# A two-layer adaLN and attention kernel: PSUM tiles dealt anew, bias products on all 128 rows, and a triangular W1 W1^T

## The chip, the cores and the metric

The kernel runs on one core of a Trainium2 chip, in one launch. The metric is the device time of that launch in microseconds (us). The profile's names are used for the engines: PE (TensorE, matrix products; PEld is its weight load), DVE (VectorE), ACT (ScalarE), POOL (GpSimd), SP (the engine whose queue issues the transfers). L905 is line 905 of the kernel. The matrix products write to PSUM, which has eight banks of 128 x 512 float32; a "PSUM tile" below is one bank. A "pass" is one matrix product with one set of weights.

## The reference, cut to what matters

The input x is 128 sequences of 64 tokens with 256 features. Layer 0 is a gated recurrence over the 64 tokens followed by a feed-forward with 8-bit fake quantisation. Layer 1 is attention and a feed-forward in hyperbolic space, modulated by a condition (adaLN), then a linear map with 6-bit block quantisation:

```python
h_new = jnp.tanh(h * leak + sigmoid(h @ Wh.T + z_t @ Wz.T + b) * z_t)      # layer 0, 64 steps
h = _act_fake_quant(jax.nn.silu(gate) * up, clip_down[0])                   # layer 0, feed-forward
x = x + jnp.einsum('bsi,hi->bsh', h, _weight_fake_quant(w_down))
...
xm = expmap0(layer_norm(logmap0(x)) * (1 + sc_msa) + sh_msa)                # layer 1, attention
q, k, v = (_to_heads(plin(xm, w, b)) for w, b in ((w_q, b_q), (w_k, b_k), (w_v, b_v)))
attn = jax.nn.softmax(einsum('bhqd,bhkd->bhqk', qt, kt) / sqrt(HD))         # 16 heads of 16
x = mobius_add(x, expmap0(g_msa * logmap0(plin(_from_heads(out_h), w_o, b_o))))
xm = expmap0(layer_norm(logmap0(x)) * (1 + sc_mlp) + sh_mlp)                # layer 1, feed-forward
ff = plin(plin(xm, w_f1, b_f1), w_f2, b_f2)
x = mobius_add(x, expmap0(g_mlp * logmap0(ff)))
...
xd = mx_dequant(mx_quant(x)); out = xd @ wd.T + bias; return x_layer0 + out
```

plin(x) is expmap0(logmap0(x) @ w + b): a linear map whose result is scaled row by row by a function of its norm. The kernel uses that for the inner plin(xm, w_f1, b_f1): the norm of u W1 + b1 is u G u^T + 2 u W1 b1 + b1 b1, with G = W1 W1^T, a symmetric 256 x 256 matrix. So the 1024-wide middle is never formed: one product with the 512 columns [G | W1 W2] gives both the norm and the result.

## The kernel before, in words

The 8192 tokens are 64 tiles of 128. Three stages follow each other. First comes the scan of the recurrence (up to about 210 us), in whose gaps the generators pieces() and products() prepare the weights: products() computes G and W1 W2 on PE and copies them from PSUM (L344), and split() stores each in two parts, so that a product is made in three passes of the float32r type. Second comes the feed-forward of layer 0 (to 308 us), which writes its hidden values to memory. Third comes the loop of fused(), which takes groups of 4 tiles, as two pairs (h2 = 0, 1), through stages that work on different groups at a time:

- front (L844): loads the hidden values, rounds them, multiplies them with w_down in PSUM tile dn (L872), adds x (L874, L875) and takes the row statistics. The product's inner length of 704 is five chunks of 128 rows and a half chunk of 64 (j = 5).
- norms (L1089): layer-norm coefficients (L656 ff.) for the attention of one group and the feed-forward of another together, then modulate (L706) and clip_ball (L720, L610).
- attention (L880): transposes of u into a qk tile, uT in two parts (L897, L898); q, k, v for two tiles in qk tiles of 512 and 256 columns (L905 the bias, L908 the six passes), copied by ACT (L910); norms of the heads (L912 to L925); scaling on POOL (L934, L938); transposes and scores in sc tiles (L959, arrays of 64 x 64), exp on ACT (L967); the result in ao (L974, 128 x 64), divided on DVE (L978, L979); transposes and the product with w_o in ao again (L1000, read by L1004).
- mlp (L1010): transposes and the product with [G | W1 W2] in ml tiles (L1026 the bias, L1029 the passes), read by DVE (L1032, the norm) and ACT (L1035, the result).
- tail (L1119): the Moebius additions of both halves (L789).
- fp6 (L1048): block quantisation, transposes and the last product in fp tiles (L1081 the bias, L1083), read by DVE (L1086).

Bias rows are added by a product of ones with the bias split into three bfloat16 rows. ones3 has 67 rows and rows3 too: the biases lie at rows 0 to 2, 32 to 34 and 64 to 66, and such a product uses 3 rows of the array.

The eight PSUM banks of the loop are two tiles for qk, two for sc, and one each for ao, ml, fp and dn. bank() takes one by its tag. The order of each engine's instructions is not the program's: a scheduler places them when the kernel is built, by priorities, dependences and the tiles that are free, and then it is fixed; each engine works its own list in order. LA = 5 and LM = 3 are the number of groups by which attention runs ahead and the last stage behind.

Of the kernel before, what the change touches and what calls it, by code (L numbers as in the profile page):

```python
# [11 lines left out]
F32 = mybir.dt.float32  # L12
F32R = mybir.dt.float32r
BF16 = mybir.dt.bfloat16
# [8 lines left out]
P = 128  # L23
B, T, D = 128, 64, 256
# [18 lines left out]
NG = NT // GN  # L43
AR = 8
TS = 4
CFG = {'rnd': 'S', 'ef': 8, 'fill': {'x1a': 'V', 'mod0': 'V'}, 'hold': [3, 0], 'mk': 3, 'mv': 6, 'xs': 3, 'la': 3, 'sb': 7, 'qks': 'GGGG', 'deq': 'VV', 'first': 1000, 'hb': 2, 'q_h': 'P', 'q_x1': 'P', 'q_xr': 'P', 'q_ot': 'P', 'q_out': 'P', 'q_ada': 'P', 'room': [[0.3, 0.3, 0.55], [0.5, 0.4, 0.2]], 'qv': 64, 'p1': 'GVGVGVGV', 'x1': 3, 'u1': 16, 'u2': 6, 'qkv': 2, 'sq': 1, 'uT1': 2, 'uT2': 2, 'qM': 2, 'kT': 2, 'e': 4, 'oT': 1, 'yT': 1, 'hq': 2, 'hl': 2, 'xr': 1, 'ot': 2, 'ada00': 2, 'ada02': 2, 'ada10': 2, 'ada12': 4, 'dn': 1, 'qk': 2, 'sc': 2, 'ao': 1, 'ml': 1, 'fp': 1, 'mod0': 'GGGV', 'mod1': 'VVVV', 'sqm0': 'SSSS', 'sqm1': 'SSSS', 'su0': 'VVVV', 'su1': 'VGVG', 'q8': 'GGGGGG', 'hqc': 'SSSVVV', 'qm': 'SSSS', 'x1a': 'GV', 'gate0': 'GGGG', 'gate1': 'GGGG', 'yb': 'GG', 'va': 'GGGG', 'sqt': 'SSSS', 'sqg': 'SSSS', 'sqo': 'SSVS', 'f2e': 'SSSS', 'early': 0, 'q8f': 'VVVVVV', 'hqf': 'SSSVVV', 'fl': 1, 'un': 2, 'jsu': 1, 'LA': 5, 'LM': 3, 'tl': 6, 'ord': 1, 'xt': 3, 'q_xt': 'P'}
GT = 4
NGR = NTILE // GT

# [21 lines left out]
def tile_kernel(ctx, tc, a, out):  # L71
# [21 lines left out]

    ones = const.tile([P, P], F32, name="ones")
    V.memset(ones, 1.0)
    ones3 = const.tile([67, P], BF16, name="ones3")
    V.memset(ones3, 1.0)

    mhead = const.tile([P, 4], F32, name="mhead")
    V.tensor_reduce(mhead, ident.rearrange("p (j v d) -> p v j d", v=4, d=HD), AX.XY, ALU.add)  # L100

    wt = ctx.enter_context(tc.tile_pool(name="wt", bufs=1))
    wqkv = wt.tile([P, 2, 2, 3 * D], F32R, name="wqkv")
    wm = wt.tile([P, 2, 2, 2 * D], F32R, name="wm")
    wo = wt.tile([P, 2, D], F32, name="wo")
    wfT = wt.tile([P, 2, D], F32, name="wfT")
# [2 lines left out]
    bf2 = wt.tile([P, D], F32, name="bf2")  # L109
    bb2 = wt.tile([P, 1], F32, name="bb2")  # L110

    rows3 = wt.tile([67, 2 * D], BF16, name="rows3")
    sdh = wt.tile([P, D], F32, name="sdh")
    cu = wt.tile([P, 1], F32, name="cu")

# [20 lines left out]
    with ExitStack() as l0:  # L136
# [15 lines left out]
        with ExitStack() as sc_:  # L152
# [173 lines left out]
            def products():  # L326

                b1T = setup.tile([P, 8], F32, name="b1T")
                dma(out=b1T, in_=a["b_f1T"])
                s1 = stage2([P, 8, D], a["w_f1T"].rearrange("(c p) k -> p c k", p=P))
                s2 = stage2([P, 8, D], a["w_f2"].rearrange("(c p) k -> p c k", p=P))
                r2 = setup.tile([1, 2 * D], F32, name="r2")
                for w, s_ in ((0, s1), (1, s2)):
                    pt = bank()
                    for c in range(2):
                        for k in range(8):
                            PE.matmul(pt[:, c * D : (c + 1) * D], lhsT=s1[:, k, c * P : (c + 1) * P],  # L340
                                      rhs=s_[:, k, :], start=(k == 0), stop=(k == 7))
                            yield 0, 0, 0.43
                    gst = setup.tile([P, 2, D], F32, name="gst", tag="gst", bufs=2)
                    S.copy(gst.rearrange("p c k -> p (c k)"), pt)  # L344
                    yield 0, 0.52, 0
                    for c in range(2):
                        sl = slice(w * D, (w + 1) * D)
                        split((wm[:, 0, c, sl], wm[:, 1, c, sl]), gst[:, c, :])
                        yield 0, 0.35, 0
                    pt = bank()  # L350
                    for k in range(8):
                        PE.matmul(pt[:1, :D], lhsT=b1T[:, k : k + 1], rhs=s_[:, k, :], start=(k == 0), stop=(k == 7))
                        yield 0, 0, 0.43
                    S.activation(r2[:, w * D : (w + 1) * D], pt[:1, :D], AF.Copy, scale=2.0 - w)
                    yield 0, 0.3, 0
                for i, part in enumerate(split3(r2, 1, G_)):
                    dma(out=rows3[64 + i : 65 + i, :], in_=part)
                bsq = setup.tile([P, 8], F32, name="bsq")
                bs1 = setup.tile([P, 1], F32, name="bs1")
                S.activation(bsq, b1T, AF.Square, accum_out=bs1)  # L360
                pt = bank()
                PE.matmul(pt[:, :1], lhsT=ones, rhs=bs1, start=True, stop=True)
                V.tensor_copy(bb2, pt[:, :1])
                yield 0.15, 0.3, 0.1


                for w in range(2):
                    st = stage2([P, 2, 3 * D], a["w_ada"].rearrange("(c p) k -> p c k", p=P)[:, :, w * 3 * D : (w + 1) * 3 * D])
                    ba = setup.tile([P, 3 * D], F32, name="ba", tag="ba", bufs=1)
                    dma(out=ba, in_=a["b_ada"][w * 3 * D : (w + 1) * 3 * D].partition_broadcast(P))  # L370
                    for q in range(3):
                        sl = slice(q * D, (q + 1) * D)
                        pt = bank()
                        for k in range(2):
                            PE.matmul(pt[:, :D], lhsT=h0T[:, k, :], rhs=st[:, k, sl], start=(k == 0), stop=(k == 1))
                            yield 0, 0, 0.43
                        if q == 1:
                            V.scalar_tensor_tensor(ba[:, sl], pt[:, :D], 1.0, ba[:, sl], ALU.add, ALU.add)
                        else:
                            V.tensor_tensor(ba[:, sl], pt[:, :D], ba[:, sl], ALU.add)  # L380
                        yield 0.35, 0, 0
                    dma(out=ada_d[:, :, w * 3 * D : (w + 1) * 3 * D],
                        in_=ba.unsqueeze(1).broadcast_to((P, AR, 3 * D)))
# [159 lines left out]
def fused(ctx, tc, a, out_tok, x_tok, L):  # L543
# [44 lines left out]
            es = CFG["fill"].get(key, es)  # L588
        return es[g % len(es)]

    def bank(tag):
        return ps.tile([P, 512], F32, name=tag, tag=tag, bufs=CFG[tag])

    def big(tag, shape, dt=F32):
        return pl.tile(shape, dt, name=tag, tag=tag, bufs=CFG[tag])
# [248 lines left out]
    def front(i):  # L844
# [4 lines left out]
        for h2 in pairs:  # L849
            pr = i0 // 2 + h2  # L850
            early = pr < CFG["early"]
            grp = pr // 2
            hs_ = slice((grp % 2) * 64, (grp % 2) * 64 + 64)
            hl = hls.pop(0)
            hq = big("hq", [P, 6, 2 * P], BF16)
            q8 = big("hb", [P, 6, 2 * P], I8)

            for e, r, j in runs("q8f" if early else "q8", hs_):
                scale(e, q8[r, j, :], hl[r, j, :], cu[r])
            for e, r, j in runs("hqf" if early else "hqc", hs_):  # L860
                if e == "V":
                    V.tensor_copy(hq[r, j, :], q8[r, j, :])
                else:
                    S.copy(hq[r, j, :], q8[r, j, :])
            load_h(pr + CFG["hl"])
            xr = big("xr", [P, 2, D])
            move("xr", out=xr, in_=x_tok[:, i0 + 2 * h2 : i0 + 2 * h2 + 2, :])
            py = bank("dn")
            for i in range(2):
                for j in range(6):  # L870
                    r = slice(0, P) if j < 5 else hs_
                    PE.matmul(py[:, i * D : (i + 1) * D], lhsT=hq[r, j, i * P : (i + 1) * P], rhs=wdT[r, j, :],  # L872
                              start=(j == 0), stop=(j == 5))
            V.tensor_tensor(x1.t[h2], two(py), bc_out(sdh, 2), ALU.mult)  # L874
            ENG[pick("x1a", h2)].tensor_tensor(x1.t[h2], x1.t[h2], xr, ALU.add)  # L875
            for g in (2 * h2, 2 * h2 + 1):
                stats(mv1[:, g, :], x1[g], 1)
            move("x1", out=x1_d[:, i0 + 2 * h2 : i0 + 2 * h2 + 2, :], in_=x1.t[h2])

    def attention(i, u, sums):  # L880
# [4 lines left out]
        for h2 in pairs:  # L885
# [13 lines left out]
            for xy in range(2):  # L899
                cs = slice(xy * P, (xy + 1) * P)  # L900
                for lo, hi in ((0, 512), (512, 768)):
                    pm = bank("qk")
                    n_ = hi - lo
                    o3 = slice(0, 3) if lo == 0 else slice(32, 35)
                    PE.matmul(pm[:, :n_], lhsT=ones3[o3, :], rhs=rows3[o3, :n_], start=True, stop=False)  # L905
                    for k in range(2):
                        for q, (w, z) in enumerate(PASSES):
                            PE.matmul(pm[:, :n_], lhsT=uT[:, z, k, cs], rhs=wqkv[:, w, k, lo:hi],  # L908
# [101 lines left out]
    def mlp(i, u, x2, sums):  # L1010
# [3 lines left out]
        for h2 in pairs:  # L1014
# [8 lines left out]
            for i in range(2):  # L1023
                g = 2 * h2 + i
                pm = bank("ml")
                PE.matmul(pm, lhsT=ones3[64:67, :], rhs=rows3[64:67, :], start=True, stop=False)  # L1026
                for k in range(2):
                    for q, (w, z) in enumerate(PASSES):
                        PE.matmul(pm, lhsT=uT[:, z, k, i * P : (i + 1) * P], rhs=wm[:, w, k, :],  # L1029
                                  start=False, stop=(k == 1 and q == 2))  # L1030
                junk3 = pl.tile([P, D], BF16, name="junk3", tag="junkz", bufs=1)
                V.tensor_tensor_reduce(out=junk3, in0=pm[:, :D], in1=u[g], scale=1.0, scalar=0.0,  # L1032
# [15 lines left out]
    def fp6(i, av, s2):  # L1048
# [4 lines left out]
        for h2 in pairs:  # L1053
# [24 lines left out]
            pm = bank("fp")  # L1078
            for i in range(2):
                o = pm[:, i * D : (i + 1) * D]  # L1080
                PE.matmul(o, lhsT=ones3[32:35, :], rhs=rows3[32:35, D:], start=True, stop=False)  # L1081
                for c in range(2):
                    PE.matmul(o, lhsT=yT[:, 2 * i + c, :], rhs=wfT[:, c, :], start=False, stop=(c == 1))  # L1083
            ot = big("ot", [P, 2, D])
# [132 lines left out]
```

## Time and profile before

| | |
|---|---|
| three runs | 1404.55, 1413.27, 1414.75 us; median 1413.27 |
| profiled execution | 1410.42 us, span 1408.5 us, mean granted PE clock 0.859 |
| scan of layer 0 | 0 to 210 us: PE busy 185.1, DVE 132.7, ACT 92.5 us |
| feed-forward of layer 0 | 210 to 308 us: PE 82.6, DVE 97.4, ACT 85.6 us |
| fused loop | 308 to 1408.5 us: PE 915.7, DVE 914.7, POOL 726.7, ACT 637.5 us |
| first and last use of ao by L974 | 398.8 and 1248.7 us |
| PE, L908 x768 | 199.4 us, mean 390 ns |
| PE, L1029 x384 | 122.6 us, mean 457 ns |
| PE, the bias products L905 x128, L1026 x64, L1081 x64 | 45.7, 26.8, 20.0 us |
| PE, L872 x384 | 72.3 us, mean 315 ns |

A row of a group gives its busy time (overlaps counted once) and the mean length of one instruction. Products on PE overlap, so their mean length is longer than the distance between their starts; the timeline gives the starts. The chain of work that ended last is followed back from the last instruction, at each step to what released it. A wait is put down to the event that ended it. The granted clock is the share of PE's full clock that the chip allowed.

### The profile page before, as it was taken

The numbers are of one execution on the slowest core, as the hardware profiler recorded it, in microseconds if no ns is written. First come the engines' busy times: TensorE is split into PE (matmuls) and PEld (weight loads), VectorE is DVE, ScalarE is ACT, GpSimd is POOL, SyncE is SP. The second block draws the span as 40 slices with busy tenths as digits, with TensorE's granted clock in tenths as the row PEclk, the third lists the DMA queues.
The fourth block names the chain that finished last, engine by engine and source line by source line (L and its number), as shares of the span: only waits on it lengthen the run. The fifth ranks groups of instructions, "written<-read, shape, count | busy, mean of one in ns | idle before, by whom it ended". The sixth has DMA issues, their size and how long they took to land.

```text
span 1408.5 us, 23861 instructions
## 1 busy us (share of the span) xinstructions
PE 1183.5 (84%) x7372; PEld 748.0 (53%) x7380; DVE 1144.8 (81%) x3604; ACT 815.5 (58%) x2363; POOL 836.6 (59%) x1043
## 2 busy tenths in 40 slices
PE   7999977974699988999889988799996999785655
PEld 4656542322466655656556565556664666553433
DVE  5666669986687988979989789979889888788863
ACT  2545447972377766667656666667765756643331
POOL 3111108865688769776685776867758764645541
PEclk9999979985599987989879899889987969976675
DMA  7113145779534234341354231532314132222111
GB/s 230 53 53 92 59 198 206 273 253 301 166 118 127 94 103 134 109 135 46 101 151 146 81 115 43 158 116 77 102 39 136 49 119 68 82 73 93 60 45 45
DMA packets 119304, 163.64 MB, mean 116 GB/s; under 512 B 10885, under 2 KB 72074, under 8 KB 119178
## 3 DMA queue, kind: packets, MB, share of 16 engines
q1 hardware_dynamic: 119178, 162.13, 36.4%
q8 instruction: 58, 0.95, 0.3%
q14 instruction: 68, 0.56, 0.1%
HBM read 115.94 MB, written 46.14 MB: 115 GB/s over the span
## 4 chain that ended last, share of the span: by engine, by line
DVE 40%; PE 35%; POOL 10%; DMA 7%; ACT 4%; issue 4%; SPq 0%; POOLq 0%; DVEq 0%; ACTq 0%
DMA ada<-ada_d 4%; PE pg L426 4%; PE qk L908 4%; PE fp L1083 4%; DVE u L789 4%; PE pg L407 3%; PE sc L959 3%; PE ml L1029 2%; PE ao L974 2%; DVE nh L913 2%; DVE bn L695 2%; DVE u L716 2%; DVE junk L735 2%; DVE u L610 2%; DVE u L1041 2%
## 5 line engine op out<-in xcount | busy, mean ns | idle before, releaser
L601 ACT ACTIVATE junk<-u 128x256 bf16<-128x256 f32 x432 | 182.2, 424 | 143.0 <-DVE u L717 46.2
L908 PE MATMUL qk<-wqkv,uT 128*128 128x512 f32 (+1 forms) x768 | 199.4, 390 | 6.3 <-DVE uT L898 3.5
L729 POOL TENSOR_TENSOR u<-u,ada 128x256 f32<-128x256 f32 x128 | 101.1, 792 | 91.7 <-ACT junk L601 88.6
L908 PEld LDWEIGHTS qk<-wqkv,uT 128*128 128x128 f32 x768 | 129.9, 207 | 46.5 <-issue 12.4
L959 PE MATMUL sc<-qM,kT 64*64 64x256 f32 x1024 | 126.7, 437 | 9.7 <-ACT kT L949 6.1
L974 PE MATMUL ao<-va,e 128*64 128x34 f32 x2048 | 93.3, 248 | 35.4 <-DVE u L979 15.3
L1029 PE MATMUL ml<-wm,uT 128*128 128x512 f32 x384 | 122.6, 457 | 0.0
L974 PEld LDWEIGHTS ao<-va,e 128*64 128x64 f32 x2048 | 83.5, 163 | 62.5 <-issue 36.3
L608 ACT ACTIVATE qM<-sc,mhead 128x256 f32<-128x256 f32 x256 | 101.3, 492 | 21.3 <-PE sc L92 21.1
L872 PE MATMUL dn<-wdT,hq 128*128 128x256 bf16 (+1 forms) x384 | 72.3, 315 | 41.3 <-DVE x L874 16.5
L938 POOL TENSOR_TENSOR va<-qkv,comb 64x256 f32<-64x256 f32 x128 | 87.2, 682 | 30.1 <-PE ao L974 24.3
L1029 PEld LDWEIGHTS ml<-wm,uT 128*128 128x128 f32 x384 | 75.5, 212 | 53.5 <-issue 35.0
L505 POOL TENSOR_TENSOR hv<-uv,sil 128x512 f32<-128x512 f32 x44 | 57.4, 1308 | 70.8 <-DVE am L508 52.2
L1083 PE MATMUL fp<-wfT,yT 128*128 128x256 f32 x256 | 92.6, 491 | 0.0
L967 ACT ACTIVATE e<-sc 128x512 f32<-128x512 f32 x128 | 73.3, 596 | 24.5 <-PE sc L959 15.1
L910 ACT COPY qkv<-qk 128x512 f32<-128x512 f32 (+1 forms) x128 | 61.3, 498 | 44.4 <-PE qk L908 43.6
L601 ACT ACTIVATION_READ_ACCUMULATOR junk<-u 128x1 f32 x432 | 86.1, 199 | 0.0
L426 PE MATMUL pg<-hsT,WT 128*128 128x128 f32 x504 | 76.3, 292 | 10.8 <-ACT hsT L438 10.4
L934 POOL TENSOR_TENSOR qkv<-qkv,comb 128x512 f32<-128x512 f32 x64 | 70.4, 1117 | 23.7 <-DVE comb L925 9.3
L426 PEld LDWEIGHTS pg<-hsT,WT 128*128 128x128 f32 x504 | 66.1, 195 | 33.3 <-ACT hsT L438 31.1
L959 PEld LDWEIGHTS sc<-qM,kT 64*64 64x64 f32 x1024 | 55.5, 147 | 48.3 <-issue 17.3
L612 POOL TENSOR_SCALAR hb<-hl,cu 128x1280 int8<-128x1280 f32 x64 | 64.8, 1018 | 23.0 <-DMA hl<-h_d 14.3
(282 smaller groups left out, 3129.7 us busy)
## 6 DMA issues: line engine op xcount, KB each, us to landing
ada<-ada_d SPq DMA_DIRECT2D x128, 256.0 KB, 3.5
h_d<-hv SPq DMA_DIRECT2D x80, 256.0 KB, 2.1
hl<-h_d SPq DMA_DIRECT2D x32, 640.0 KB, 5.1
ada<-ada_d SPq DMA_DIRECT2D x128, 128.0 KB, 2.6
xt<-in_xT_dram SPq DMA_DIRECT2D x16, 512.0 KB, 4.1
xr<-in_x_dram SPq DMA_DIRECT2D x32, 256.0 KB, 3.7
x_d<-x SPq DMA_DIRECT2D x32, 256.0 KB, 2.4
xt<-x_d SPq DMA_DIRECT2D x32, 256.0 KB, 2.7
```

The costliest lines, as they stand in the source:

```text
L426: lp = PE.matmul(pg[c][:, st], lhsT=WT[:, k, c * P : (c + 1) * P], rhs=hp[:, k, :], start=False, stop=False, skip_group_check=True)
L601: S.activation(junk, src, AF.Square, accum_out=acc)
L608: S.activation(dst, src, AF.Copy, scale=by)
L729: ENG[pick(f"gate{which}", g)].tensor_tensor(av, av, gb, ALU.mult)
L872: PE.matmul(py[:, i * D : (i + 1) * D], lhsT=hq[r, j, i * P : (i + 1) * P], rhs=wdT[r, j, :], start=(j == 0), stop=(j == 5))
L908: PE.matmul(pm[:, :n_], lhsT=uT[:, z, k, cs], rhs=wqkv[:, w, k, lo:hi], start=False, stop=(k == 1 and q == 2))
L938: ENG[pick("va", g)].tensor_tensor(va[r, :, s, 0:HD], qkv[r, xy, 512:768].rearrange("p (h d) -> p h d", d=HD), bc_in(comb[r, xy * 48 + 32 ...
L959: PE.matmul(sc[rr][s * T : (s + 1) * T, c * 256 : (c + 1) * 256].rearrange("p (v t) -> p v t", v=4), lhsT=kTs[xy][r, c, s * T : (s + 1) * ...
L967: S.activation(e.rearrange("p c v t -> p (c v t)"), sc[rr], AF.Exp, scale=1.0 / math.sqrt(HD))
L974: PE.matmul(pv[xy * T : (xy + 1) * T, hh], lhsT=E[2 * xy + hh // 4][:, c, hh % 4, :], rhs=vas[(2 * h2 + xy) % 4][:, c * 8 + hh], start=Tru ...
L1029: PE.matmul(pm, lhsT=uT[:, z, k, i * P : (i + 1) * P], rhs=wm[:, w, k, :], start=False, stop=(k == 1 and q == 2))
L1083: PE.matmul(o, lhsT=yT[:, 2 * i + c, :], rhs=wfT[:, c, :], start=False, stop=(c == 1))
```

## The change

The diff, with the long dictionary of settings cut to the entries that differ:

```diff
-CFG = {... 'dn': 1, 'qk': 2, 'sc': 2, 'ao': 1, 'ml': 1, 'fp': 1, ...}
+CFG = {... 'qk': 2, 'sc': 2, 'ao': 2, 'm': 2, ...}
...
-    ones3 = const.tile([67, P], BF16, name="ones3")
-    V.memset(ones3, 1.0)
+    ones3 = const.tile([P, 3, P], BF16, name="ones3")
+    V.memset(ones3, 0.0)
+    for n in range(3):
+        V.memset(ones3[32 * n : 32 * n + 3, n, :], 1.0)
...
-    rows3 = wt.tile([67, 2 * D], BF16, name="rows3")
+    rows3 = wt.tile([P, 2 * D], BF16, name="rows3")
+    V.memset(rows3, 0.0)
...
                     S.copy(gst.rearrange("p c k -> p (c k)"), pt)
-                    yield 0, 0.52, 0
+                    if w == 0:
+                        S.activation(gst[:, 0, P:], pt[:, P:D], AF.Copy, scale=2.0)
+                    yield 0, 0.52 + 0.3 * (1 - w), 0
...
-    def bank(tag):
-        return ps.tile([P, 512], F32, name=tag, tag=tag, bufs=CFG[tag])
+    def bank(name):
+        tag = "m" if name in ("ml", "fp", "dn") else name
+        return ps.tile([P, 512], F32, name=name, tag=tag, bufs=CFG[tag])
...
-            for i in range(2):
-                for j in range(6):
-                    r = slice(0, P) if j < 5 else hs_
-                    PE.matmul(py[:, i * D : (i + 1) * D], lhsT=hq[r, j, i * P : (i + 1) * P], rhs=wdT[r, j, :],
-                              start=(j == 0), stop=(j == 5))
+            for i, j in [(i, j) for i in range(2) for j in range(5)] + [(0, 5), (1, 5)]:
+                r = slice(0, P) if j < 5 else hs_
+                PE.matmul(py[:, i * D : (i + 1) * D], lhsT=hq[r, j, i * P : (i + 1) * P], rhs=wdT[r, j, :],
+                          start=(i == 0 and j == 0), stop=(j == 5), skip_group_check=True)
...
-                    o3 = slice(0, 3) if lo == 0 else slice(32, 35)
-                    PE.matmul(pm[:, :n_], lhsT=ones3[o3, :], rhs=rows3[o3, :n_], start=True, stop=False)
+                    PE.matmul(pm[:, :n_], lhsT=ones3[:, lo // 512, :], rhs=rows3[:, :n_], start=True, stop=False)
...
-                PE.matmul(pm, lhsT=ones3[64:67, :], rhs=rows3[64:67, :], start=True, stop=False)
+                PE.matmul(pm, lhsT=ones3[:, 2, :], rhs=rows3, start=True, stop=False)
                 for k in range(2):
+                    cs = slice(k * P, 2 * D)
                     for q, (w, z) in enumerate(PASSES):
-                        PE.matmul(pm, lhsT=uT[:, z, k, i * P : (i + 1) * P], rhs=wm[:, w, k, :],
+                        PE.matmul(pm[:, cs], lhsT=uT[:, z, k, i * P : (i + 1) * P], rhs=wm[:, w, k, cs],
                                   start=False, stop=(k == 1 and q == 2))
...
-                PE.matmul(o, lhsT=ones3[32:35, :], rhs=rows3[32:35, D:], start=True, stop=False)
+                PE.matmul(o, lhsT=ones3[:, 1, :], rhs=rows3[:, D:], start=True, stop=False)
```

In words: the eight banks become two each for qk, sc and ao, and two ("m") that ml, fp and dn share. The weights of the bias products are zero outside the three rows of their bias, so the products use all 128 rows. In front, the ten products with whole chunks come first and the two half chunks after them. G is symmetric: its upper right quarter is doubled when it is copied, and the passes of the second half of u (k = 1) leave out the lower left quarter, so they have 384 columns and not 512. The scheduler works on the changed program, so the order on every engine is another too.

More of the change, by code (lines that the diff above doesn't have):

```diff
@@ L45 @@
 TS = 4
-CFG = {'rnd': 'S', 'ef': 8, 'fill': {'x1a': 'V', 'mod0': 'V'}, 'hold': [3, 0], 'mk': 3, 'mv': 6, 'xs': 3, 'la': 3, 'sb': 7, 'qks': 'GGGG', 'deq': 'VV', 'first': 1000, 'hb': 2, 'q_h': 'P', 'q_x1': 'P', 'q_xr': 'P', 'q_ot': 'P', 'q_out': 'P', 'q_ada': 'P', 'room': [[0.3, 0.3, 0.55], [0.5, 0.4, 0.2]], 'qv': 64, 'p1': 'GVGVGVGV', 'x1': 3, 'u1': 16, 'u2': 6, 'qkv': 2, 'sq': 1, 'uT1': 2, 'uT2': 2, 'qM': 2, 'kT': 2, 'e': 4, 'oT': 1, 'yT': 1, 'hq': 2, 'hl': 2, 'xr': 1, 'ot': 2, 'ada00': 2, 'ada02': 2, 'ada10': 2, 'ada12': 4, 'dn': 1, 'qk': 2, 'sc': 2, 'ao': 1, 'ml': 1, 'fp': 1, 'mod0': 'GGGV', 'mod1': 'VVVV', 'sqm0': 'SSSS', 'sqm1': 'SSSS', 'su0': 'VVVV', 'su1': 'VGVG', 'q8': 'GGGGGG', 'hqc': 'SSSVVV', 'qm': 'SSSS', 'x1a': 'GV', 'gate0': 'GGGG', 'gate1': 'GGGG', 'yb': 'GG', 'va': 'GGGG', 'sqt': 'SSSS', 'sqg': 'SSSS', 'sqo': 'SSVS', 'f2e': 'SSSS', 'early': 0, 'q8f': 'VVVVVV', 'hqf': 'SSSVVV', 'fl': 1, 'un': 2, 'jsu': 1, 'LA': 5, 'LM': 3, 'tl': 6, 'ord': 1, 'xt': 3, 'q_xt': 'P'}
+CFG = {'rnd': 'S', 'ef': 8, 'fill': {'x1a': 'V', 'mod0': 'V'}, 'hold': [3, 0], 'mk': 3, 'mv': 6, 'xs': 3, 'la': 3, 'sb': 7, 'qks': 'GGGG', 'deq': 'VV', 'first': 1000, 'hb': 2, 'q_h': 'P', 'q_x1': 'P', 'q_xr': 'P', 'q_ot': 'P', 'q_out': 'P', 'q_ada': 'P', 'room': [[0.3, 0.3, 0.55], [0.5, 0.4, 0.2]], 'qv': 64, 'p1': 'GVGVGVGV', 'x1': 3, 'u1': 16, 'u2': 6, 'qkv': 2, 'sq': 1, 'uT1': 2, 'uT2': 2, 'qM': 2, 'kT': 2, 'e': 4, 'oT': 1, 'yT': 1, 'hq': 2, 'hl': 2, 'xr': 1, 'ot': 2, 'ada00': 2, 'ada02': 2, 'ada10': 2, 'ada12': 4, 'qk': 2, 'sc': 2, 'ao': 2, 'm': 2, 'mod0': 'GGGV', 'mod1': 'VVVV', 'sqm0': 'SSSS', 'sqm1': 'SSSS', 'su0': 'VVVV', 'su1': 'VGVG', 'q8': 'GGGGGG', 'hqc': 'SSSVVV', 'qm': 'SSSS', 'x1a': 'GV', 'gate0': 'GGGG', 'gate1': 'GGGG', 'yb': 'GG', 'va': 'GGGG', 'sqt': 'SSSS', 'sqg': 'SSSS', 'sqo': 'SSVS', 'f2e': 'SSSS', 'early': 0, 'q8f': 'VVVVVV', 'hqf': 'SSSVVV', 'fl': 1, 'un': 2, 'jsu': 1, 'LA': 5, 'LM': 3, 'tl': 6, 'ord': 1, 'xt': 3, 'q_xt': 'P'}
 GT = 4
```

## The prediction

> **What bounds the kernel now.** I read the page's engine shares and chain first, then a table by stage, then TensorE's own timeline, then who waits for whom. The first two lines are the page's busy times and the shares of the chain that ended last; the next three are the table of stretches after the feed-forward of layer 0 (308 us): filling, full loop, draining. Columns: stretch, length, busy us and count for PE, PEld, DVE, ACT, POOL, then granted clock, DMA share, GB/s.
>
> ```profile
> PE 1183.5 (84%) x7372; PEld 748.0 (53%) x7380; DVE 1144.8 (81%) x3604; ACT 815.5 (58%) x2363; POOL 836.6 (59%) x1043
> ...
> DVE 40%; PE 35%; POOL 10%; DMA 7%; ACT 4%; issue 4%; SPq 0%; POOLq 0%; DVEq 0%; ACTq 0%
> ```
> ```profile
> 308.00:420.00 112.00, 74.92 (x425) 44.11 (x424) 81.64 (x229) 44.92 (x109) 74.71 (x111) 0.68 0.68 197
> 420.00:1300.00 880.00, 772.61 (x5529) 516.15 (x5528) 767.00 (x2558) 561.80 (x1715) 612.91 (x762) 0.87 0.33 100
> 1300.00:1408.50 108.50, 68.20 (x197) 40.33 (x195) 66.06 (x261) 30.76 (x94) 39.11 (x41) 0.66 0.16 49
> ```
>
> Two engines share the bound: in the 880 us of full loop PE is busy 88% and DVE 87%. Adding up the pieces of the chain after 308 us gives DVE 501, PE 305, POOL 135, DMA 78 us. So a third of PE's 916 busy us there sets the end. Now PE's timeline in a dense stretch at full clock (start, length, line, tiles, shape of the array used, result, count):
>
> ```profile
> 639.81 1.08 PE L959 MATMUL sc<-qM,kT 64*64 64x256 f32 x8
> 640.83 0.38 PE L905 MATMUL qk<-rows,ones 3*128 3x512 bf16 x1
> 641.14 1.66 PE L908 MATMUL qk<-wqkv,uT 128*128 128x512 f32 x6
> 642.74 0.28 PE L905 MATMUL qk<-rows,ones 3*128 3x256 bf16 x1
> 642.94 0.98 PE L908 MATMUL qk<-wqkv,uT 128*128 128x256 f32 x6
> 643.76 1.89 PE L1000 MATMUL ao<-wo,oT 128*128 128x256 f32 x8
> 645.48 0.60 PE L92 MATMUL qk<-ident,u 128*128 128x128 f32 x4
> 646.01 0.38 PE L1026 MATMUL ml<-rows,ones 3*128 3x512 bf16 x1
> 646.33 1.67 PE L1029 MATMUL ml<-wm,uT 128*128 128x512 f32 x6
> 647.94 0.39 PE L905 MATMUL qk<-rows,ones 3*128 3x512 bf16 x1
> 648.25 0.73 PE L908 MATMUL qk<-wqkv,uT 128*128 128x512 f32 x2
> 648.91 0.31 PE L974 MATMUL ao<-va,e 128*64 128x34 f32 x4
> ```
>
> Starts are what counts. The run of six 512-column passes takes 641.14 to 642.74, 1.60 us; the run of two, 648.25 to 648.91, 0.66 us. Both follow a 3-row bias product and end at a change of array shape, so four more passes cost 0.94, 0.235 each, and the ends of a run cost 0.66 - 0.47 = 0.19 us. The bias product itself holds PE 0.32 (640.83 to 641.14), 0.085 above a pass of its width. Likewise at 256 columns: 0.82 for six passes with no change behind them (642.94 to 643.76), about 0.12 each and 0.10 over; the bias product 0.20, 0.08 over. So a 3-row product among 128-row work costs three times about 0.1 us: going in, coming out, and once more after the first pass back, where the next weights are late. Last, the waits that end at a PSUM tile (who waited for whom: us, times, longest):
>
> ```profile
> PE dn L872 <- DVE x L874: 16.5, 9, 4.0
> PE ao L974 <- DVE u L979: 15.3, 6, 6.8
> PE ao L974 <- DVE u L1004: 11.2, 6, 3.3
> PE ml L92 <- ACT u L1035: 7.0, 5, 3.1
> PE ml L1026 <- ACT u L1035: 4.9, 6, 1.8
> ```
> ```profile
> DVE ot L1086 <- PE fp L1083: 22.7, 10, 6.6
> DVE junk L1032 <- PE ml L1029: 18.6, 14, 5.1
> DVE rden L978 <- PE ao L974: 15.2, 11, 2.9
> ```
>
> **The change part by part.** The sum is made against the profiled execution's own 1410.4 us, 2.9 below the median of the three runs. All prices are at full clock.
>
> *Bias products on 128 rows.* 128 for qk, 64 for ml, 64 for fp. In the built order 203 of these 256 are entered from 128-row work, so coming out and the late weights go 256 times, 51 us, and going in 203 times, 20 us: 71 us. The product's columns are as many as before.
>
> *Half chunks together.* Changes between 128-row and 64-row shapes fall from 62 in and 50 out to 32 and 31 in the built order: 49 x 0.1 = 5 us. All changes of shape in the loop fall from 879 to 311, some 60 more than these two edits explain, by longer runs: 6 us.
>
> *No lower quarter.* 192 passes lose 128 of 512 columns. Between the two widths above a column costs (0.235 - 0.12)/256 = 0.45 ns: 11 us.
>
> Together PE loses 93 of 916 us of work. Of that I count the share that is on the chain: its pieces at L905, L1026 and L1081 are 28 of these lines' 92 busy us, at L1029 34 of 123. 0.30 x 93 = **28 us**; none of it counts if DVE is always next, all if PE alone bounds.
>
> [...]
>
> *PSUM tiles.* A second ao tile lets the second half of the heads start while DVE still reads the first (L979) and the transposes while it reads the last product (L1004): 15.3 + 11.2 + 6.7 (the transposes' own wait) = 33 us of PE idle, a third on the chain, 11, of which I take 9. ml may put its second tile's products beside the first's reading: waits on L1035 are 12 us, so 4. Against it, ml, fp and dn now share two tiles, and in PE's fixed order everything behind the waiting matmul stands too (qk, sc, ao, so ACT's copies and POOL's scalings). If each of 32 dn and 32 fp results waited for one eviction of 0.68 us (L874, L1086), 44 us, a third is 15; if none did, 0. I take 5, nearer the lower end: 12 uses a group, each some 1.6 us of products and 0.7 of reading with the copies between, make about 30 of the 116 us that two tiles offer in a group's 58 us (L925 at 586 and at 1195 us, 21 pairs apart). Net -8, between -13 and +15.
>
> *The order that follows.* In the built order dn no longer runs two groups ahead but half a group, since it must get a shared tile, and after the last ao result 9 pairs of ml and 14 of fp remain, where 7 and 11 did. One more group is drained in a stretch where DVE is busy 68% (1249 us to the end) and not 88%: its 31 us of DVE work take 46 and not 35. Bounds 0 and +11; I take **+8**, since there two ml tiles are free of sc and ao's competition.
>
> *Clock.* Between the full loop (PE 88%, clock 0.87) and the drain (63%, 0.66) the clock falls by 0.8 points for each point of PE busy. With 93 us of work gone and 24 of time, PE's share falls by up to 7 points, the clock by 0.055, and its 822 us grow by 53, a third on the chain: +16. If the idle time stays in pieces like today's, 0. I take **+4**. [...]
>
> *Small things.* Four more memsets on DVE lie before 7.6 us, where PE waits for its first input and DVE has 4 us idle; without that cover at most 4 x 0.48 (the longest memset) = 2 us. One ACT copy of 128x128 in the scan, about 0.3 us, lies beside ACT's 56% idle there; uncovered, 0.3. Transfers are the same in kind and number, and one queue carries them.
>
> Sum: -28 - 8 + 8 + 4 = -24: **1386 us**.
>
> **The rivals.** *DVE swallows it.* DVE is busy 87%, has half the chain, and its work stays. Its idle time ended by PE (22.7 + 18.6 + 15.2 = 57 us) shrinks only as PE's work does, 10%: 6 us less, and the drain gives that back: about 1408. For it: DVE's share; against: PE idles just 12% in the full loop, so DVE can't hide all of PE.
>
> *PE was the real brake.* All of these 57 us go: 1354. For it: DVE waits for PE on all three; against: part of them lies in the drain, where latency rules.
>
> *The short lead of dn makes it slower.* In the new order a group's dn stands about 26 us of PE work ahead of that group's first transposes. Between lie L874 0.68, L875 on POOL 1.35, statistics 1.0, the coefficients (small DVE operations 4.5, two POOL powers 3.4, ACT 0.6), three tiles of modulate on POOL at 2.3 = 6.9, a square 0.6, the radius on POOL 2.4, the clip 1.0: 22.4 us without any queue. POOL also has a pair's scalings in between (2 x 1.12 + 4 x 0.68 = 5.0). It decides once queues add more than 3.6 us to each group; at 4 us over, 11 full groups lose 44: 1430. For it: POOL and DVE are 70% and 87% busy, the same order every group; against: much of POOL's list can run while DVE computes.
>
> **How the numbers follow.** Three runs of this kernel spread over 10 us, so about 1% (14 us, 1399 to 1427) can be told from no change. Forecast (1370 to 1399) 0.42; PE the brake (under 1370) 0.24; DVE swallows (1399 to 1427) 0.15; short lead (over 1427) 0.19. Faster 0.66, same 0.15, slower 0.19. The range 1340 to 1430 takes in the three rivals' points and leaves out some 0.05 below and 0.12 above.
>
> **What would show it.** Right: no 3-row matmul after 308 us and 128-row passes evenly 0.235 apart; PE busy after 308 us near 830 to 870; waits of ao on L979 and L1004 nearly gone; DVE over 88% busy in the full loop. Wrong: DVE below 87% with POOL's L632, L712 to L714 or L729 ending its waits (short lead); dn or fp waiting for L1086, L874 or L1032 by more than 44 us (too few shared tiles); the clock under 0.82 in the full loop.

## The result, and the profile after

The changed kernel takes 1518.31 us (median; 1514.18 to 1522.33), the kernel before 1409.66 us in the same comparison: 1.077 times as long, interval 1.071 to 1.083. The forecast was 1386 us, a gain; the change is a loss.

The profiled execution took 1521.9 us, with a span of 1520.1. Busy times and the chain that ended last, from the page of the changed kernel:

```profile
PE 1163.0 (77%) x7354; PEld 782.2 (51%) x7380; DVE 1141.2 (75%) x3608; ACT 822.4 (54%) x2364; POOL 828.8 (55%) x1043
...
DVE 34%; PE 28%; POOL 18%; DMA 7%; ACT 6%; issue 6%; SPq 0%; POOLq 0%; DVEq 0%; ACTq 0%
```

The table by stage after the feed-forward of layer 0 (columns as before: stretch, length, busy us and count for PE, PEld, DVE, ACT, POOL, then granted clock, DMA share, GB/s):

```profile
308.00:420.00 112.00, 72.74 (x491) 47.09 (x492) 85.76 (x245) 49.51 (x122) 81.30 (x117) 0.74 0.68 201
420.00:1300.00 880.00, 694.15 (x4985) 496.87 (x4999) 670.48 (x2187) 508.32 (x1521) 534.76 (x675) 0.79 0.28 87
1300.00:1520.00 220.00, 131.41 (x654) 92.57 (x654) 156.11 (x613) 86.17 (x276) 101.71 (x123) 0.76 0.24 75
```

DVE has the same work as before after 308 us (912 and 915 us), but in the full loop it is busy 76% of the time and not 87%, PE 79% and not 88%. No engine fills the time, POOL's share of the chain has grown from 10% to 18%, and the granted clock is 0.79 where it was 0.87. The loop has slowed to a wait.

What the change was written for did happen. PE's timeline in the full loop (start, length, line):

```profile
932.21 0.39 PE L1035 MATMUL ml<-rows,ones 128*128 128x512 bf16 x1
932.25 1.58 PE L1039 MATMUL ml<-wm,uT 128*128 128x512 f32 x6
933.66 1.09 PE L917 MATMUL qk<-wqkv,uT 128*128 128x512 f32 x4
```

No 3-row product is left. A bias product with its six passes now takes 1.45 us (932.21 to 933.66) where it took 1.93 (646.01 to 647.94 before); of the difference, the columns left out are 0.17 (three passes, 128 columns, 0.45 ns each). The waits that the ao tile caused are gone as well: of 33 us, 0.7 are left on L988 (L979 before) and none on L1013 (L1004). The new waits are elsewhere (who waited for whom in the full loop: us, times, longest):

```profile
POOL u L739 <- ACT junk L611: 99.9, 63, 5.2
POOL cfq L655 <- DVE fn L1042: 63.1, 10, 8.6
PEld sc L968 <- ACT kT L958: 61.5, 45, 4.8
...
POOL suq L655 <- ACT junk L611: 40.9, 11, 5.9
```

POOL waits once in each group, 6.3 us on average, for the norm that DVE takes from ml (L1042), then works off what had piled up behind it in its own list.

**The circle.** Three timelines of the changed kernel over one group. First PE's:

```profile
1004.63 1.58 PE L1039 MATMUL ml<-wm,uT 128*128 128x512 f32 x6
...
1007.81 2.46 PE L882 MATMUL dn<-wdT,hq 128*128 128x256 bf16 x19
...
1013.01 0.82 PE L882 MATMUL dn<-wdT,hq 128*128 128x256 bf16 x5
...
1062.88 0.27 PE L92 MATMUL ml<-ident,u 128*128 128x128 f32 x1
...
1079.54 1.57 PE L1039 MATMUL ml<-wm,uT 128*128 128x512 f32 x6
...
1082.71 2.46 PE L882 MATMUL dn<-wdT,hq 128*128 128x256 bf16 x19
```

DVE's, from the reading of dn's second half to the clip before the next ml (in brackets: idle before, and its releaser):

```profile
1013.51 4.09 DVE L1051 SCALAR_TENSOR_TENSOR u<-u,cfr,bf 128x256 f32<-128x256 f32 x4 [0.90 <-POOL cfr L657]
1017.52 0.68 DVE L884 TENSOR_TENSOR x<-dn,sdh 128x512 f32<-128x512 f32 x1
...
1022.09 0.71 DVE L705 BATCH_NORM_STATS2 bn<-x 128x6 f32<-128x256 f32 x2
...
1046.84 0.48 DVE L727 SCALAR_TENSOR_TENSOR u<-u,lnaln,ada 128x256 f32<-128x256 f32 x1
...
1055.15 0.48 DVE L727 SCALAR_TENSOR_TENSOR u<-u,lnaln,ada 128x256 f32<-128x256 f32 x1
...
1059.98 2.56 DVE L620 TENSOR_SCALAR u<-u,sur 128x256 f32<-128x256 f32 x6 [1.99 <-POOL sur L657]
```

And POOL's:

```profile
1027.83 1.66 POOL L642 TENSOR_TENSOR rnln<-x2sln,nhalf 128x8 f32<-128x8 f32 x1 [2.60 <-DVE x2sln L676]
...
1035.90 2.90 POOL L642 TENSOR_TENSOR r<-q,nhalf 128x16 f32<-128x16 f32 x1
1038.76 1.64 POOL L642 TENSOR_TENSOR lnaln<-tln,nhalf 128x8 f32<-128x8 f32 x1
1040.71 2.14 POOL L722 TENSOR_SCALAR u<-x,nm,lnaln 128x256 f32<-128x256 f32 x3 [0.31 <-DVE lnaln L700]
...
1050.66 0.93 POOL L723 TENSOR_TENSOR u<-u,ada 128x256 f32<-128x256 f32 x1 [3.62 <-DMA ada<-ada_d]
...
1056.68 1.67 POOL L642 TENSOR_TENSOR sur<-suq,nhalf 128x8 f32<-128x8 f32 x1
```

Read them as one story. The last ml products of a turn start at 1004.63; dn of the newest group follows at 1007.81, for it gets a shared tile only after ml's. Its second half is read at 1017.52, though its last products start at 1013.01: in DVE's list this reading stands behind L1051, which waits for the factor that POOL makes of ml's norm. So DVE's order ties dn to ml as well as PE's. The statistics (L705) end at 1022.8. POOL takes the first root at 1027.83, as soon as DVE has its argument, and the second (lnaln) at 1038.76, 4 us after its argument, behind other work of its list such as the 2.90 us of r. Modulate begins on POOL at 1040.71. The half for ml is modulated by 1047.3 (L727 at 1046.84), but the radius is taken for both halves at once and waits for the attention's, where POOL stands still for 3.62 us until the condition is loaded (L723; 41 us in 11 such waits in the full loop). The radius comes at 1056.68, the clip at 1059.98, and at 1062.88 PE transposes for ml. That is ml of the *next* turn: norms() computes one set of coefficients and radii for both halves, the attention of group k+5 and the feed-forward of group k, so ml waits for the statistics of the newest dn. After it dn starts again, at 1082.71, 74.9 us later. Of these, 55 us go from dn to ml and 20 from ml to dn. (From 711 to 1227 us dn starts eight groups, 74 us apart on average.) Before, a group took 58 us.

### The profile page after: what moved, and what is told of

Its sections match the earlier page's. It is cut to its first block, busy times and chain, and to the rows that moved or that the text cites. A ratio compares the mean times of both kernels' runs of the same rounds, so it can differ in the third digit from the quotient of the medians.

```text
span 1520.1 us, 23939 instructions
## 1 busy us (share of the span) xinstructions
PE 1163.0 (77%) x7354; PEld 782.2 (51%) x7380; DVE 1141.2 (75%) x3608; ACT 822.4 (54%) x2364; POOL 828.8 (55%) x1043
## 4 chain that ended last, share of the span: by engine, by line
DVE 34%; PE 28%; POOL 18%; DMA 7%; ACT 6%; issue 6%; SPq 0%; POOLq 0%; DVEq 0%; ACTq 0%
PE ml L1039 5%; PE pg L434 4%; PE qk L917 3%; PE pg L415 3%; POOL r L642 3%; DMA ada<-ada_d 3%; POOL va L947 3%; DVE u L1051 3%; DVE u L799 2%; POOL qkv L943 2%; DVE junk L745 2%; DVE u L726 2%; DVE u L727 2%; PE ao L1009 2%; DMA xt<-x_d 2%
## 5 line engine op out<-in xcount | busy, mean ns | idle before, releaser
L968 PE MATMUL sc<-qM,kT 64*64 64x256 f32 x1024 | 172.1, 498 | 41.9 <-ACT kT L958 37.5
L917 PE MATMUL qk<-wqkv,uT 128*128 128x512 f32 (+1 forms) x768 | 178.8, 373 | 6.7 <-DVE uT L908 3.4
L739 POOL TENSOR_TENSOR u<-u,ada 128x256 f32<-128x256 f32 x128 | 97.9, 765 | 145.5 <-ACT junk L611 122.8
L968 PEld LDWEIGHTS sc<-qM,kT 64*64 64x64 f32 x1024 | 72.9, 166 | 114.4 <-ACT kT L958 67.9
L983 PEld LDWEIGHTS ao<-va,e 128*64 128x64 f32 x2048 | 97.2, 175 | 62.3 <-issue 22.2
L983 PE MATMUL ao<-va,e 128*64 128x34 f32 x2048 | 107.1, 259 | 24.9 <-ACT e L976 24.0
L1039 PE MATMUL ml<-wm,uT 128*128 128x512 f32 (+1 forms) x384 | 110.2, 426 | 7.2 <-ACT uT L1030 6.2
L1009 PE MATMUL ao<-wo,oT 128*128 128x256 f32 x256 | 82.6, 479 | 14.2 <-ACT oT L1004 14.0
L922 DVE TENSOR_REDUCE nh<-sq 128x48 f32<-128x768 f32 x64 | 60.4, 944 | 37.2 <-ACT sq L921 37.0
L1093 PE MATMUL fp<-wfT,yT 128*128 128x256 f32 x256 | 83.0, 461 | 2.4 <-ACT yT L1087 2.3
L882 PE MATMUL dn<-wdT,hq 128*128 128x256 bf16 (+1 forms) x384 | 61.0, 305 | 30.4 <-DVE nm L1107 11.2
```

The lines of the kernel that those rows point to most:

```text
L739: ENG[pick(f"gate{which}", g)].tensor_tensor(av, av, gb, ALU.mult)
L968: PE.matmul(sc[rr][s * T : (s + 1) * T, c * 256 : (c + 1) * 256].rearrange("p (v t) -> p v t", v=4), lhsT=kTs[xy][r, c, s * T : (s + 1) * ...
L983: PE.matmul(pv[xy * T : (xy + 1) * T, hh], lhsT=E[2 * xy + hh // 4][:, c, hh % 4, :], rhs=vas[(2 * h2 + xy) % 4][:, c * 8 + hh], start=Tru ...
L1009: PE.matmul(pm[:, i * D : (i + 1) * D], lhsT=oT[:, 2 * i + c, :], rhs=wo[:, c, :], start=(c == 0), stop=(c == 1))
L1039: PE.matmul(pm[:, cs], lhsT=uT[:, z, k, i * P : (i + 1) * P], rhs=wm[:, w, k, cs], start=False, stop=(k == 1 and q == 2))
```

## The experiments

Times are medians, ratios to the kernel before in the same comparison. The first four tell apart dn's place (theory lead), the number of tiles (tiles) and the 128-row and other product edits (products). dn's place is counted in the built order of the full loop: how many pairs of tiles dn runs ahead of its own attention's transposes; 4 to 6 in the kernel before, 0 to 1 in the changed one.

**psum_only.** The kernel before with the shared tiles alone:

```diff
-CFG = {... 'dn': 1, 'ao': 1, 'ml': 1, 'fp': 1, ...}
+CFG = {... 'ao': 2, 'm': 2, ...}
-    def bank(tag):
+    def bank(name):
+        tag = "m" if name in ("ml", "fp", "dn") else name
...
```

> The kernel before with the new PSUM tiles alone (two ao tiles, two shared by ml, fp and dn); its products are the old ones. Theory 'lead' (the shared tiles are handed out in the program's order, so a group's dn comes 0 to 1 pair ahead of its own attention instead of 4 to 6, and the loop waits for the chain from dn to the transposes): 1500 to 1560 us, a period of 70 us or more. Theory 'tiles' (two tiles are too few for three stages, wherever dn stands): 1500 to 1560 us too. Theory 'products' (the new products, or the order that they happen to bring, cost the time): about 1410 us.

1605.78 us, ratio 1.138 (1.133 to 1.143); dn 0 to 2 pairs ahead. More than any theory gave; the last runs return to it.

**products_only.** The changed kernel with the old tiles (the reverse of the diff above); dn 4 to 6 pairs ahead.

> The changed kernel with the PSUM tiles of before (one each for ao, ml, fp, dn): 128-row bias products, half chunks together, no lower quarter. Theories 'lead' and 'tiles': 1370 to 1400 us, PE's saved 93 us of work paying a third. Theory 'products': 1480 to 1520 us.

1384.81 us, ratio 0.981 (0.977 to 0.984). The product edits are a gain of 28 us by themselves, and the loss lies in the tiles and what follows from them.

**whole_front_first.** The whole change, with front called before mlp in a turn, so that dn is given its tile before ml of that turn; dn 2 to 3 pairs ahead:

```diff
+        if k + LA + CFG["fl"] < NGR:
+            front(k + LA + CFG["fl"])
         if 0 <= k < NGR:
             mlp(k, ums[k], us[k], sums(k + LM, HM))
         if k + LA < NGR:
             attention(k + LA, uas[k + LA], sums(k + LA, HA))
-        if k + LA + CFG["fl"] < NGR:
-            front(k + LA + CFG["fl"])
```

> The changed kernel, tiles shared as in it, but front is called before mlp in the program, so that dn gets its shared tile earlier; in the built order dn stands 2 to 3 pairs ahead. Theory 'lead': 1390 to 1430 us. Theory 'tiles': still 1490 to 1530 us. Theory 'products': still 1490 to 1530 us.

1424.78 us, ratio 1.010 (1.006 to 1.014): the same tiles, the same work, 94 us less.

**products_dn_late.** products_only, tiles as before the change, but dn's products are made to follow the last ml products on PE; dn 0 to 1 pairs ahead:

```diff
-                PE.matmul(py[...], lhsT=hq[...], rhs=wdT[r, j, :], ...)
+                with tc.issue_after(last[0].ins) if last[0] else nullcontext():
+                  PE.matmul(py[...], lhsT=hq[...], rhs=wdT[r, j, :], ...)
...
-                        PE.matmul(pm[:, cs], ...)
+                        last[0] = PE.matmul(pm[:, cs], ...)
```

> products_only with its five separate kinds of tiles, but dn's products are held back on PE until the last ml product of the same turn of the loop, so that dn stands 0 to 1 pair ahead as in the changed kernel. Theory 'lead': 1470 to 1530 us with a period of 70 us or more. Theory 'tiles': as products_only, within 1%. Theory 'products': as products_only.

1552.23 us, ratio 1.099 (1.096 to 1.103). The order alone, with no tile shared, costs 167 us over products_only, 22 us more than the upper end of theory lead. The same stretch of the full loop, first of products_only, then of products_dn_late:

```profile
420.00:1150.00 730.00, 603.36 (x4813) 439.18 (x4811) 652.06 (x2103) 482.05 (x1465) 528.98 (x661) 0.88 0.35 105
```
```profile
420.00:1150.00 730.00, 541.94 (x4147) 395.02 (x4145) 542.52 (x1736) 421.05 (x1240) 434.33 (x542) 0.78 0.29 88
```

DVE falls from 89% to 74% busy, with the same instructions: the picture of the changed kernel, made without its tiles. Of the three theories for this loss, lead stands, and tiles and products fall.

**Which tiles may be shared.** In the next three dn has a tile of its own or the shared ones are three:

```text
 whole_dn_own:        'dn': 1, 'm': 1, 'ao': 2, and dn taken out of the shared tag
 whole_dn_own_ao1:    'dn': 1, 'm': 2, 'ao': 1, the same
 whole_three_shared:  'm': 3, 'ao': 1, dn shared as in the change
```

> The whole change, but dn has a PSUM tile of its own again; ml and fp share one tile, the attention's result keeps two. In the built order dn then stands 4 to 7 pairs ahead of its own attention, as in the kernel before. Theory lead (only dn's place costs): 1370 to 1400 us, near products_only's 1385, and lower by up to 9 if the second ao tile is worth what the prediction took. Rival sharing (waiting for one another's shared tile costs too, here more than in the whole change, since ml and fp have one tile and not two): over 1430.

1466.86 us, ratio 1.040 (1.035 to 1.046).

> The whole change, but dn has a tile of its own, ml and fp share two, and the attention's result has one tile as before. dn stands 4 to 7 pairs ahead. Theory lead: 1375 to 1400. Beside whole_dn_own it prices the second ao tile against a second shared tile: if the prediction's 9 us for the ao tile hold, whole_dn_own is lower by about 5 to 10; if ml and fp's sharing costs more, it is higher.

1380.74 us, ratio 0.979 (0.976 to 0.983).

> The whole change, but three tiles shared by dn, ml and fp, and one for the attention's result. Number of tiles as in the kernel before, only handed out in turn; in the built order dn stands 1 to 2 pairs ahead of its own attention (0 to 1 in the whole change, 2 to 3 in whole_front_first). Theory lead: between those two, 1440 to 1500. Rival tiles (two shared tiles are too few, three are enough): under 1420.

1522.45 us, ratio 1.080 (1.076 to 1.084).

whole_dn_own_ao1 is as expected: with dn alone, ml and fp on two tiles cost nothing (1381 beside 1385). The other two are misses. whole_dn_own is over the rival's 1430: one tile for ml and fp costs 82 us although dn is 4 to 7 pairs ahead. And whole_three_shared, with dn 1 to 2 pairs ahead, should have come between 1440 and 1500 by theory lead, and is as slow as the change. The count of pairs is not the right measure.

**whole_dn_own_m1_ao1**, whole_dn_own with 'ao': 1, tells the two causes of the first miss apart:

> whole_dn_own with one ao tile (one bank unused): dn has its own tile, ml and fp share one. It tells what whole_dn_own's 82 us over products_only are. If ml and fp's one tile costs them: 1450 to 1480 here too (by the prediction's 9 us for the second ao tile, some 9 more than whole_dn_own). If the second ao tile did it by the order that it allows: near 1385.

1463.47 us, ratio 1.039 (1.034 to 1.043). It is the single tile of ml and fp; beside it a second ao tile is worth nothing (1467 and 1463). Two waits of its fp transposes from 420 us to the end, which products_only has at 6.5 us (L1096) and not at all (L1045):

```profile
PE fp L92 <- DVE ot L1096: 19.9, 12, 3.2
...
PE fp L92 <- ACT u L1045: 13.1, 10, 3.6
```

fp waits until ml's result is copied, so the two stages take turns. But in products_only the same transposes wait for their own input instead (L1080, 29.7 us; 8.2 here), so these waits sum to 41 and 36 us, and by which path the single tile costs 79 us stays open.

**bias_only.** The kernel before with the 128-row bias products (the lines of ones3 and rows3 in the diff) and nothing else:

> The kernel before with the 128-row bias products alone. By the prediction's terms 71 of the 93 us of TensorE work are theirs and 30% of it counts: 21 us less than the kernel before, about 1391. Rival (the half chunks, the quarter or the longer runs carry what products_only gained): over 1402.

1387.28 us, ratio 0.983 (0.979 to 0.988): 22.7 us less, against 21 expected.

**Durations or loads.** If the circle sets the pace, a shorter piece of it must show, even where it adds work. Every root is taken on ACT and DVE and none on POOL:

```diff
-        if src.shape[1] <= len_pow:
+        if tag == "never":
             G_.tensor_tensor(dst, src, nhalf[:, : src.shape[1]], ALU.pow)
             return
```

> The whole change, with every reciprocal root taken on ACT and DVE (logarithm, exponential, three small DVE operations) instead of POOL's power. dn stands 0 to 1 pairs ahead as in the whole change. In the whole change's trace POOL's powers take 1.05, 2.9, 1.6 and 1.7 us in the chain that one group hands to the next; the replacement takes about 1.2 each. Theory lead (the 73 us of a group are a serial chain of durations, no engine's load): about 2.5 us or more a group, 11 or 12 groups, so 25 to 50 us less than the whole change: 1468 to 1493, although DVE and ACT get some 50 us more work. Rival load (some engine's work sets the pace): not below 1518, by DVE's added work rather above.

1485.56 us, ratio 1.053 (1.049 to 1.058): 33 us less than the changed kernel, inside the 25 to 50 of theory lead, with 50 us more DVE work (1190.8 and 1141.2 us).

> products_only with the same edit of the roots; dn stands 4 to 6 pairs ahead. Theory lead: here DVE's load counts (88% busy in the full loop) and the chain's length hardly: six roots a group at 0.6 us of DVE, about 55 us more DVE work, of which 40% is on the chain: 0 to 25 us more than products_only, 1385 to 1410. Rival (the powers' latency or POOL's load slows every order alike): 25 to 50 less, about 1345 to 1360.

1354.7 us, ratio 0.962 (0.958 to 0.966): a miss; 30 us less than products_only where theory lead gave 0 to 25 more. So the roots' latency counts in the early order too, and this pair doesn't tell the theories apart; my picture of that order as bound by DVE's load alone was wrong. DVE's work also grew by 20 us only (1167.5 and 1147.1), where I had expected 55. The groups of the root of 16 columns, in the changed kernel (420 to 1300 us) and in whole_quick_roots (420 to 1150 us; busy, mean ns of one | idle before):

```profile
L642 POOL TENSOR_TENSOR r<-q,nhalf 128x16 f32<-128x16 f32 x13 | 37.8, 2909 | 3.0 <-DVE rh L932 1.6 <-DVE q L755 0.8
```
```profile
L648 DVE SCALAR_TENSOR_TENSOR rs<-rs,q 128x16 f32<-128x16 f32 x11 | 3.6, 327 | 0.2
...
L649 DVE SCALAR_TENSOR_TENSOR r<-rs,r 128x16 f32<-128x16 f32 x11 | 2.7, 248 | 0.2
...
L645 ACT ACTIVATE r<-q 128x16 f32<-128x16 f32 x11 | 2.6, 237 | 10.4 <-DVE q L755 10.4
L646 ACT ACTIVATE r<-r 128x16 f32<-128x16 f32 x11 | 2.5, 230 | 0.2
...
L647 DVE TENSOR_TENSOR rs<-r 128x16 f32<-128x16 f32 x11 | 2.2, 197 | 8.7 <-ACT r L646 8.7
```

One operation of 2.9 us is replaced by five that add up to 1.24, the gaps between them left out.

**Opening the circle.** By the three timelines it closes at norms(). There the two halves are now computed apart, the feed-forward's before mlp, the attention's after it; tiles and order rules stay:

```diff
-            norms(k, xss.get(k))
+            norms(k, xss.get(k), 1)
         if done and CFG["ord"] == 1:
             fp6(k - LM, *done)
         if 0 <= k < NGR:
             mlp(k, ums[k], us[k], sums(k + LM, HM))
+        norms(k, None, 0)
         if k + LA < NGR:
...
-        x2n, la = ln_coeffs(mv, xs)
+        x2n, la = ln_coeffs(mv[:, h, :], xs[:, h] if which and xs is not None else None, which)
...
+        clip_ball(u, radial(un, f"su{which}"), which)
```

> The whole change (dn, ml and fp on two shared tiles, two ao tiles), but the layer-norm coefficients and the radii of the two halves are computed apart: the feed-forward's before mlp, the attention's after it. Then ml of a turn needs nothing of the newest dn, and the circle ml, dn, statistics, norms, ml is open although dn still stands behind ml of the same turn. Theory circle: the 133 us over products_only go, and the split's own price comes on top (about 25 small DVE operations and two POOL powers more a group, some 70 us of DVE work, a part of it on the chain): between products_split_norms and 40 us above it, under 1460. Rival (dn's place itself costs, by whatever waits for it): at or above the whole change, 1515 or more.

1366.04 us, ratio 0.969 (0.965 to 0.972): 152 us less than the changed kernel, with more instructions. Theory circle expected a time between products_split_norms (1393, below) and 40 us above it; the gain is larger than that by 27 us.

> products_only with the norms split in the same way: the price of the split where dn has its own tile. 70 us more DVE work at 40% on the chain: 1385 plus 10 to 35, about 1395 to 1420; less if the wait of ml for the newest dn's statistics counted there too.

1393.21 us, ratio 0.990 (0.987 to 0.993): the split alone costs 8 us (13 by the two ratios) where the circle was open anyway, about the lower end of the 10 to 35 expected. The full loop of whole_split_norms, over the same stretch as above:

```profile
420.00:1150.00 730.00, 622.91 (x4851) 442.73 (x4848) 662.29 (x2361) 487.38 (x1489) 547.88 (x711) 0.89 0.34 103
```

DVE is back at 91%, the clock at 0.89; the starts of dn's groups lie 60 us apart (nine groups from 590 to 1074 us). dn still stands behind all 24 ml products of the same turn, and mostly 2 to 3 pairs ahead. That is more than in the changed kernel, but whole_front_first has the same 2 to 3 pairs and takes 59 us longer. So it is not dn's place as such, but that ml waits for what dn yields. This explains whole_three_shared: ml of a turn takes six tiles, so dn with three tiles still follows ml of the same turn (in its trace too dn stands behind all 24 products); and whole_front_first: there dn follows ml of the turn before, and the circle has two turns of time.

**What the rest is worth with the circle open.** psum_only with the same split of norms():

> psum_only (the new PSUM tiles with the 3-row bias products, the old half chunks and the full product with G) with the norms split in two, so that the circle is open. Against whole_split_norms (1366) it prices the three product edits. Theory circle: with the circle open they are worth what they were with dn alone, about 28 us: 1385 to 1405. Rival (shared tiles by themselves make the products dearer): the 88 us between the whole change and psum_only stay: about 1454.

1403.7 us, ratio 0.993 (0.989 to 0.998). With the circle open the product edits are worth 38 us (1403.7 against 1366.0; 35 by the ratios), with it closed 88 (1605.8 against 1518.3): nearer the 28 of products_only, as the theory said. So of the 93 us of PE work that the edits were reckoned to save, nearly all shows in the closed circle and 30 to 40% outside it; by which steps the circle takes in nearly all isn't traced.

**Do the gains add up?** whole_dn_own_ao1, then whole_split_norms, each with the edit of the roots:

> whole_dn_own_ao1 (dn alone, ml and fp on two tiles, one ao tile) with the roots on ACT and DVE. If the gains add up as in products_quick_roots: 1381 less 30, about 1350; the fastest of the study or level with products_quick_roots.

1353.16 us, ratio 0.960 (0.956 to 0.964): as expected, and with products_quick_roots (1354.7) the fastest of the study, 4% under the kernel before.

> whole_split_norms with the roots on ACT and DVE. If the roots' 30 us add to the open circle: about 1336, the fastest of the study; if DVE's added work (some 10 roots a group now) swallows them: near 1366 or above.

1401.25 us, ratio 0.992 (0.988 to 0.996): the second case, 35 us over whole_split_norms. The gains don't add up; the runs don't show whether DVE's work alone (1199 us in all, the most of the study) does it or the new order.

## Why the prediction was wrong

- *Product edits, -28: right.* In products_only PE is busy 824.16 us after 308 us, against 915.73: 91.6 us removed where 93 were worked out. Of these 27.7 came off the time, 30%, the share read from the chain. bias_only took 73 us from PE, where 71 were predicted, and 23 off the time, where 21 were. The half chunks and the quarter make up the rest, 18 us of PE work and 5 of time (22 and 7 predicted); neither was run alone. The weights of 128 rows took hardly longer to load: 98 ns at the median in the changed kernel (L1035 on PEld, 64 loads) and 90 with 3 rows (L1026, 64 loads). From a bias product to the second pass behind it go 0.47 us (932.21 to 932.67) where 0.66 went (646.01 to 646.67), both at full clock.
- *PSUM tiles, -8: the bounds of the waits held, the scope was wrong.* The ao waits went, and dn and fp wait 32 us for shared tiles (L884 7.1, and of fp's first products L884 12.6 and L1096 12.2), under the 44 that I took as the bound, but twice the 15 of which my 5 were a third. With the circle open, the new tiles even gain 27 us (whole_split_norms against products_split_norms), more than my best end of 13. The traces place the gain in the drain, which I had taken to get longer: from the last L934 to the end are 173 and 214 us, while the time up to it is no shorter (1186 and 1177). Which tile gives it is open, since beside a single ml and fp tile the second ao tile gave nothing. But I priced a shared tile only as a wait for an eviction. It also fixes an order.
- *Order, +8: the step that failed.* I saw that dn moved from two groups ahead to half a group, and costed of that only the longer drain. The drain didn't change: from the last L934 (L925 before) to the end are 204 us after and 213 before. What the move cost was 16 us in every full group (74 and 58); the changed kernel has eight such groups, from 639 to 1227 us, so some 125 of the 133 us over products_only.
- *The rival "short lead" had the place and the signs* (DVE at 76%, POOL's roots and L739 in the chain) *but not the price: 4 us a group, 1430 us, 0.19.* I set 22.4 us of work against a lead of 26 us and asked by how much queues would exceed it. The way from dn to ml takes 55 us in the trace, so by that count 33 of them go to queues and waits for other inputs. And I took it for a race that is lost by a few us; I didn't ask whether the end of the chain leads back to its start. It does, through norms() and the shared tiles, and then the whole sum, 75 us, is the period. Both parts of it could be read before the run: the joint coefficients in norms(), and in the built order that dn comes after ml.
- *Clock, +4.* With the circle open the clock didn't fall: 0.88 in the full loop in products_only as in the kernel before, with PE at 83% and 89%. With it closed it fell to 0.79, and the same products keep PE busy for 898 us after 308 us and not 824. How much of the 133 us comes by way of the clock, the runs don't separate. My +4 lay between an estimate of 16 and a 0 for idle time that stays in pieces as before; no run shows that 0 or the +4 by itself. What the runs showed is a clock that stayed (0.88) or fell by 0.09.
- *DVE swallows it, PE the real brake:* products_only at 1385 lies between both, where the forecast had its own term.

## What to carry to other kernels

A shared tile pool was an order as well as a resource here: it was handed out in program order, so a producer that had run ahead was tied to the consumer before it (dn fell from 4 to 6 pairs ahead to 0 to 1; called before mlp, it stood 2 to 3 ahead). Before sharing, follow the moved product's result forward and see whether it reaches, within the same turn, the stage that must release its tile; if it does, the sum of that chain, queues included, is the new period (here 75 us, where a group took 58). Such a circle can be opened at a joint computation that mixes early and late inputs (here at a price of 8 us for a gain of 152), or by giving the producer its own tile again (whole_dn_own_ao1, 138 us).

## What the runs showed of the hardware

- The record of the granted clock has two values alone in the traces of the kernel before and of the changed one, full and half (1000 and 399 us before, 952 and 558 us changed), so a mean between them is a share of time. How often it is half went, in one pair, with the shape of PE's idle time rather than its share. psum_only and products_only both have PE busy 82 to 83% from 420 to 1150 us, with clocks of 0.77 and 0.88. Counted in the trace over that stretch, PE's idle pieces over 2 us are 30 and 16 (11 in the kernel before, with a clock of 0.88, and 30 in the changed one, with 0.79); in all runs here those with at most 20 have clocks of 0.84 to 0.91, those with 24 or more 0.76 to 0.79. No experiment changed the pieces alone, so this is a relation and not a cause. It hangs on the length counted, too: of pieces over 3 us products_only has 11, with a clock of 0.88, and whole_quick_roots 10, with 0.79.
- POOL's power took longer the more columns it had: 1.05 to 1.11 us at 4, 1.64 to 1.68 at 8, 2.9 at 16 on 128 rows (L642 in the changed kernel), while the five operations that replace it add up to 1.24 us at 16 columns.
